# Turning the adjacency of the first three pairs on TensorE, and a new layout for the later pairs

## The chip, the cores and the metric

The kernel runs on one core of one Trainium2 chip. The metric is the device time of one execution in microseconds (us). Every kernel was checked against the reference on the chip, and all of them were correct.

## The reference, cut to what matters

```python
# x, adj: 64 graphs of 256 nodes x 256 features, float32
xc = transpose(x)
h = relu(bn(conv1d(xc, conv1_w)))
h = bn(conv1d(h, conv2_w, pad=8))              # 17 taps
x_conv = transpose(relu(h + xc))
s = x @ w_se.T + b_se                          # 3 numbers a node
dist = ...                                     # squared distances of the rows of s
A = exp(-dist) * adj                           # the mask is adj
msg = relu(x @ w_msg.T + b_msg)
x_nmp = einsum('bnm,bmd->bnd', A, msg)
gi, gh = concat(x_conv, x_nmp) @ w_ih.T + b_ih, x @ w_hh.T + b_hh
... GRU gates on gi, gh and x ...
```

The sum over m needs A with m on the partitions, that is, A turned. exp(-dist) is symmetric, so it is enough to turn adj ahead of the multiply, or the product behind it.

## The kernel before

Two graphs are a pair, four pairs are a batch, and there are eight batches. The 17-tap convolution is done by transforms: filters are made once from `taps`, stored to DRAM (`filt`) and loaded again as `wb` for the products of each batch. The program opens with a preamble (taps arrive, conv1 and the filters of the first batch), then runs the batches.

adj takes a road through DRAM. It is turned by transposing DMAs as 16-bit halves, stored (kept), loaded, and joined to float32 by two ScalarE copies:

```python
def turn_adj(i):
    HALVES[i] = (part of T, a buffer of the preamble) if i < 2 else late.tile(..., name="halves")
    for g in range(G):                                   # 2 transposing DMAs a pair
        nc.sync.dma_start_transpose(out=HALVES[i][:, g], in_=adj[G * i + g].bitcast(U16))
def keep_adj(i):                                         # 8 stores of 64 KB, rows of 512 B
    ...
def load_adj(i):                                         # 8 loads of 64 KB, issued by SP
    ...
def join_adj(i):
    for j in range(2):
        nc.scalar.copy(v[:, j], ADJH[i][:, :, :, j]...)
def affinity(i, early=False):
    ...                                                  # e = exp(-dist) on ScalarE
    nc.vector.tensor_mul(e, e, ADJ[i]...)                # times adj
def aggregate(i, join=True):                             # x_nmp; E is the moving operand
    mm(graph(p, g), MSG[i][...], E[i][:, g, c, :], ...)
    if join: join_adj(i + 1)
```

The schedule, cut to the opening and the first batch:

```python
turn_adj(0); turn_adj(1)
for j in range(PB):                          # 4 steps of the preamble
    transpose_h(j)                           # also loads x of pair j + 2: by ScalarE for j < 2, else by SP
    conv1(j); run(split_steps(j))
    for m, n in steps[j * 4:(j + 1) * 4]:
        filters(m, n, nc.sync)               # matmul, ScalarE copy to fo, store by SP
    if j < 2: keep_adj(j)
...                                          # remaining filters, stored by SP and GpSimd in turn
load_adj(0); join_adj(0)
for b in range(NB):
    message(i); products(b, 0); embed(i); products(b, 1); affinity(i)
    load_adj(i + 1); products(b, 2) ...
    aggregate(i)
    if b == 0: (load w_hh and w_ih, 2.3 MB, by GpSimd)
    message(i + 1) ... embed(i + 1); affinity(i + 1)
    if b == 0: turn_adj(2)
    products(b, 6)
    if b == 0: keep_adj(2); turn_adj(3)
    ...
    if b == 0: load_adj(2); keep_adj(3)
    aggregate(i + 1, b > 0); ... embed(i + 2)
    gates(i, 0, wait, early)                 # early: join_adj(2) if b == 0, then affinity(i + 2)
    load_adj(i + 3); turn_adj(nxt)
    if b == 0: load_y(0); load_y(1)
    ...
```

## Time and profile before

| | before |
|---|---|
| median of 4 runs | 1957.59 us (1954.89 to 1958.72) |
| span of the profiled run | 1956.3 us |
| mean granted TensorE clock | 0.977 |
| TensorE busy | 1849.5 us, 95% |
| ScalarE / GpSimd busy | 644.7 / 136.1 us |
| DMA packets | 230,650 |

The profile is of one execution. PE is TensorE, PEld its weight loads, DVE VectorE, ACT ScalarE, POOL GpSimd, SP the engine that issues most DMAs; a q behind a name (SPq) is that engine's queue of DMA issues. A line in order of time reads: start, length, engine, source line, operation, output and inputs, count, and in brackets the idle time just before and what ended it. TensorE is the bound, so what to read is its idle time: 64 of its 106.8 us lie in the first 245 us. The prediction shows those lines. In what follows h is the output of the first convolution, fo the buffer in which ScalarE puts a finished group of filters before it is stored, and y the input x as the GRU reads it again.

### The profile page before, as it was taken

How to read it: one execution, taken by the hardware profiler on the slowest of the kernel's cores; microseconds unless marked ns; L12 is line 12 of the kernel's file. 1: busy time of each engine (PE TensorE's matmuls, PEld its weight loads, DVE VectorE, ACT ScalarE, POOL GpSimd, SP SyncE). 2: the span in 40 equal slices, each digit the busy share in tenths (PEclk: the TensorE clock that was granted, in tenths of full speed). 3: DMA queues.
4: the chain of work that ended last, by engine and by line, in shares of the span. 5: the costliest groups of instructions: out<-in, count | busy, mean ns of one | idle time of the engine just before them, and what ended most of it. 6: DMA issues, size and time to landing. Idle time of an engine off the chain costs nothing.

```text
span 1956.3 us, 22266 instructions
## 1 busy us (share of the span) xinstructions
PE 1849.5 (95%) x7684; PEld 1143.7 (58%) x7684; DVE 1396.9 (71%) x2667; ACT 644.7 (33%) x1338; POOL 136.1 (7%) x204
## 2 busy tenths in 40 slices
PE   2979899999999999999999999999999999999997
PEld 1659454684448654594547744486546844477443
DVE  1758756998389865898469874898659994698522
ACT  0532343244222442224322433234422353224321
POOL 2110000000000001000000000000000000000000
PEclk8989899999999999999999999999999999998999
DMA  7777531372316514183414723165232723153020
GB/s 144 226 243 215 141 91 50 98 241 57 85 43 202 160 50 91 44 249 80 102 38 121 230 54 81 45 210 144 60 80 62 242 80 86 22 163 118 1 43 22
DMA packets 230650, 220.75 MB, mean 113 GB/s; under 512 B 90114, under 2 KB 160514, under 8 KB 230537
## 3 DMA queue, kind: packets, MB, share of 16 engines
q1 hardware_dynamic: 205516, 175.45, 31.3%
q0 software_dynamic: 20576, 40.21, 8.3%
q10 hardware_dynamic: 4445, 3.67, 0.7%
q8 instruction: 61, 1.00, 0.2%
q14 instruction: 52, 0.43, 0.1%
HBM read 156.54 MB, written 45.88 MB: 103 GB/s over the span
## 4 chain that ended last, share of the span: by engine, by line
PE 73%; DVE 11%; DMA 6%; ACT 5%; issue 4%; POOL 0%; SPq 0%; ACTq 0%; DVEq 0%; POOLq 0%
PE acc L447 63%; PE aux L447 6%; DMA wb<-filt 3%; PE aux L451 2%; DMA taps<-in_c_wT_dram 2%; PE aux L734 1%; ACT Yv L68 1%; DVE T L65 1%; DVE Yv L59 1%; DVE Yv L62 1%; ACT adj L423 1%; DVE U L65 1%; DVE PT L62 1%; DVE Sv L62 1%; DVE T L62 1%
## 5 line engine op out<-in xcount | busy, mean ns | idle before, releaser
L447 PE MATMUL acc<-hT,w_hh 128*128 128x512 f32 x768 | 365.3, 611 | 0.0
L447 PE MATMUL acc<-xnm,w_ih 128*128 128x512 f32 x768 | 354.5, 598 | 0.0
L447 PE MATMUL acc<-Yv,w_ih 128*128 128x512 f32 x768 | 340.2, 592 | 0.0
L447 PEld LDWEIGHTS acc<-xnm,w_ih 128*128 128x128 f32 x768 | 148.4, 193 | 189.2 <-issue 187.5
L447 PEld LDWEIGHTS acc<-Yv,w_ih 128*128 128x128 f32 x768 | 145.7, 190 | 184.2 <-issue 182.1
L447 PEld LDWEIGHTS acc<-hT,w_hh 128*128 128x128 f32 x768 | 145.5, 195 | 167.3 <-issue 163.0
L783 ACT ACTIVATE tr<-acc,b_rz 128x512 f32<-128x512 f32 x64 | 44.0, 687 | 552.0 <-PE acc L447 552.0
L785 DVE SCALAR_TENSOR_TENSOR gn<-tr,gn 128x512 f32<-128x512 f32 x64 | 44.2, 691 | 245.7 <-ACT tr L783 245.7
L447 PE MATMUL acc<-hT,w_c 128*128 128x512 f32 x256 | 117.8, 603 | 18.6 <-ACT hT L580 18.6
L447 PE MATMUL acc<-V,wb 128*128 128x128 f32 x1024 | 127.0, 277 | 3.5 <-DMA wb<-filt 3.3
L447 PE MATMUL aux<-w_msg,hT 128*128 128x259 f32 x512 | 121.7, 385 | 6.8 <-DVE msg L706 6.8
L447 PEld LDWEIGHTS acc<-V,wb 128*128 128x128 f32 x1024 | 121.2, 194 | 4.2 <-DMA wb<-filt 4.2
L447 PE MATMUL acc<-U,wb 128*128 128x128 f32 x1024 | 122.9, 276 | 0.0
L447 PEld LDWEIGHTS acc<-U,wb 128*128 128x128 f32 x1024 | 119.3, 192 | 3.6 <-issue 2.7
L59 DVE SCALAR_TENSOR_TENSOR V<-T,V 128x256 f32<-128x256 f32 (+2 forms) x224 | 120.4, 607 | 0.3
L447 PE MATMUL aux<-e,msg 128*128 128x256 f32 x512 | 115.8, 379 | 0.0
L447 PEld LDWEIGHTS aux<-w_msg,hT 128*128 128x128 f32 x512 | 94.5, 190 | 30.2 <-DVE msg L706 13.3
L811 POOL DMA_DIRECT2D out_dram<-y x64 | 39.4, 619 | 968.9 <-DVE y L810 939.9
L447 PEld LDWEIGHTS aux<-e,msg 128*128 128x128 f32 x512 | 95.5, 190 | 15.9 <-issue 4.3
L447 PEld LDWEIGHTS acc<-hT,w_c 128*128 128x128 f32 x256 | 48.3, 192 | 69.4 <-issue 43.2
L423 ACT COPY adj<-adjh 128x1024 uint16<-128x1024 uint16 x64 | 81.3, 1339 | 19.9 <-DMA adjh<-halves_d 14.7
L65 DVE TENSOR_TENSOR V<-h 128x512 f32<-128x512 f32 x64 | 43.8, 685 | 61.6 <-ACT h L593 61.4
(131 smaller groups left out, 2512.6 us busy)
## 6 DMA issues: line engine op xcount, KB each, us to landing
wb<-filt SPq DMA_DIRECT2D x376, 256.0 KB
adjh<-halves_d SPq DMA_DIRECT2D x256, 64.0 KB
y<-in_x_dram POOLq DMA_DIRECT2D x64, 256.0 KB, 5.8
out_dram<-y POOLq DMA_DIRECT2D x64, 256.0 KB, 5.1
x<-in_x_dram SPq DMA_DIRECT2D x60, 256.0 KB
halves_d<-halves SPq DMA_DIRECT2D x240, 64.0 KB
filt<-fo SPq DMA_DIRECT2D x26, 252.0 KB
filt<-fo POOLq DMA_DIRECT2D x10, 252.0 KB, 5.9
```

Of the source, the lines that this page charges most:

```text
L59: return self.step(out, lambda: self.v.scalar_tensor_tensor(out, x, s, y, op0=ALU.mult, op1=ALU.add))
L62: return self.step(out, lambda: self.v.tensor_add(out, x, y))
L65: return self.step(out, lambda: self.v.tensor_sub(out, x, y))
L68: return 0, lambda: self.a.mul(x, x, s)
L423: nc.scalar.copy(v[:, j], ADJH[i][:, :, :, j].rearrange("p g c n -> p (g c) n"))
L447: nc.tensor.matmul(p, w, v, **kw)
L451: nc.tensor.transpose(p, v, ident)
L734: nc.tensor.matmul(p[:, :N], ZT[rows_q, :P], ZT[rows_q, P:], start=True, stop=True)
L783: nc.scalar.activation(tr, pr, AF.Tanh, bias=b_rz[:, dc:dc + 1], scale=0.5)
L785: nc.vector.scalar_tensor_tensor(gn, tr, 1.0, gn, op0=ALU.add, op1=ALU.mult)
L811: nc.gpsimd.dma_start(out=rows(out, G * i + g), in_=row_tile(Y[i], g))
```

## The change

The intent is to take adj off the path in the opening. For the first three pairs adj is loaded as it is, and TensorE transposes the product A. From pair 3 on, one transposing DMA turns both graphs of a pair, rows are 1 KB, there are 4 stores and 4 loads a pair instead of 8 and 8, and GpSimd issues the loads. The diff, cut to its core:

```diff
+    BY_DMA = 3
     def turn_adj(i):
-        (into T if i < 2)
-        for g in range(G):
-            nc.sync.dma_start_transpose(out=HALVES[i][:, g], in_=adj[G * i + g].bitcast(U16))
+        HALVES[i] = late.tile([P, 2 * MC, W], U16, name="halves")
+        nc.sync.dma_start_transpose(out=HALVES[i], in_=adj[G * i:G * (i + 1)]...bitcast(U16))
     def keep_adj(i):
-        (8 stores, 512-byte rows)
+        for k in range(2 * MC):
+            nc.sync.dma_start(out=v[k], in_=HALVES[i][:, k])
-    def load_adj(i):
-        (8 loads by nc.sync)
+    def load_adj(i, eng=nc.gpsimd):
+        if i < BY_DMA:
+            load_rows(ADJ[i], adj, i, eng)
+            return
+        for q in range(2 * MC):
+            eng.dma_start(out=ADJH[i][:, q], in_=ADJD[i][:, q])
     def affinity(i, early=False):
...
+        AT[i] = E[i]
+        if i + 1 < BY_DMA:
+            load_adj(i + 1)
+    def transpose_a(i):
+        AT[i] = late.tile([P, 2 * MC, W], U16, name="adjh")...        # the buffer of adjh
+        for g in range(G):
+            q = aux()
+            (4 transposes of 128x128 of E[i] into q)
+            nc.scalar.copy(AT[i][:, g]..., q)
...
-    turn_adj(0)
-    turn_adj(1)
+    load_adj(0, nc.sync)
...
-        if j < 2:
-            keep_adj(j)
...
-    load_adj(0)
-    join_adj(0)
...  first batch: transpose_a(0) after products 2, transpose_a(1) after products 6,
...  transpose_a(2) after the first gates; turn_adj(3), keep_adj(3) ahead of aggregate(1)
```

More of the change, by code (lines that the diff above doesn't have):

```diff
@@ L390, in turn_adj @@
             return
-        if i < 2:
-            HALVES[i] = Tt.bitcast(U16).rearrange("p (i g k n) -> p i g k n", i=2, g=G, n=N)[:, i]
-        else:
-            HALVES[i] = late.tile([P, G, 2 * MC, N], U16, name="halves")
-        for g in range(G):
-            nc.sync.dma_start_transpose(out=HALVES[i][:, g], in_=adj[G * i + g].bitcast(U16))
+        HALVES[i] = late.tile([P, 2 * MC, W], U16, name="halves")
+        nc.sync.dma_start_transpose(out=HALVES[i],
+                                    in_=adj[G * i:G * (i + 1)].rearrange("g n m -> (g n) m").bitcast(U16))
     def keep_adj(i):
@@ L400, in keep_adj @@
             return
-        ADJD[i] = dram.tile([G, L // 2, MC, 2, NW, N], U16, name="halves_d", bufs=6)
-        v = ADJD[i].rearrange("g h c j (k a) n -> g k a (h c j) n", a=4)
-        for g in range(G):
-            for k in range(2 * MC):
-                nc.sync.dma_start(out=v[g, k], in_=HALVES[i][:, g, k])
-    def load_adj(i):
+        ADJD[i] = dram.tile([L // 2, 2 * MC, NW, W], U16, name="halves_d", bufs=6)
+        v = ADJD[i].rearrange("h q (k a) n -> k a (h q) n", a=4)
+        for k in range(2 * MC):
+            nc.sync.dma_start(out=v[k], in_=HALVES[i][:, k])
+    def load_adj(i, eng=nc.gpsimd):
         if i >= B // G:
             return
-        ADJH[i] = late.tile([P, G, MC, 2, N], U16, name="adjh")
-        v = ADJD[i].rearrange("g h c j b n -> g c j h b n")
-        for g in range(G):
-            for c in range(MC):
-                for j in range(2):
-                    nc.sync.dma_start(out=ADJH[i][:, g, c, j], in_=v[g, c, j])
+        if i < BY_DMA:
+            ADJ[i] = work.tile([P, G * MC, N], FP, name="adj")
+            load_rows(ADJ[i], adj, i, eng)
+            return
+        ADJH[i] = late.tile([P, 2 * MC, W], U16, name="adjh")
+        for q in range(2 * MC):
+            eng.dma_start(out=ADJH[i][:, q], in_=ADJD[i][:, q])
     def join_adj(i):
-        if i >= B // G:
+        if not BY_DMA <= i < B // G:
             return
         ADJ[i] = work.tile([P, G * MC, N], FP, name="adj")
-        v = ADJ[i].bitcast(U16).rearrange("p q (n j) -> p j q n", j=2)
+        v = ADJ[i].bitcast(U16).rearrange("p (g c) (n j) -> p j c g n", g=G, j=2)
+        u = ADJH[i].rearrange("p (c j) (g n) -> p j c g n", j=2, g=G)
         for j in range(2):
-            nc.scalar.copy(v[:, j], ADJH[i][:, :, :, j].rearrange("p g c n -> p (g c) n"))
+            nc.scalar.copy(v[:, j], u[:, j])
     def load_y(i):
@@ L454 @@
     PSUM, ACT = 0.2, 0.9
-    HT, MSG, E, XNM = {}, {}, {}, {}
+    HT, MSG, E, AT, XNM = {}, {}, {}, {}, {}
     def norm_steps(i):
@@ L741, in affinity, with aggregate @@
                 nc.vector.tensor_mul(e, e, ADJ[i][:, g * MC + c].rearrange("p (b h c) -> p c h b", c=MC, b=NW))
-    def aggregate(i, join=True):
+        AT[i] = E[i]
+        if i + 1 < BY_DMA:
+            load_adj(i + 1)
+    def transpose_a(i):
+        AT[i] = late.tile([P, 2 * MC, W], U16, name="adjh").bitcast(FP).rearrange("p a (b n) -> p a b n", n=N)
+        AT[i] = AT[i].rearrange("p a b n -> p (a b) n").rearrange("p (g c) n -> p g c n", g=G)
+        for g in range(G):
+            q = aux()
+            for c in range(MC):
+                for r in range(MC):
+                    transpose(q[:, c * N + r * P:c * N + (r + 1) * P], E[i][:, g, r, c * P:(c + 1) * P])
+            nc.scalar.copy(AT[i][:, g].rearrange("p c n -> p (c n)"), q)
+    def aggregate(i):
         XNM[i] = late.tile([P, DC, W], FP, name="xnm", bufs=2)
@@ L748, in aggregate @@
                 for c in range(MC):
-                    mm(graph(p, g), MSG[i][:, g, c, dc * P:(dc + 1) * P], E[i][:, g, c, :], N,
+                    mm(graph(p, g), MSG[i][:, g, c, dc * P:(dc + 1) * P], AT[i][:, g, c, :], N,
                        start=(c == 0), stop=(c == MC - 1))
             nc.scalar.activation(XNM[i][:, dc, :], p, AF.Copy)
-        if join:
-            join_adj(i + 1)
+        join_adj(i + 1)
     OT = {}
@@ L887 @@
         affinity(i)
-        load_adj(i + 1)
+        if b > 0:
+            load_adj(i + 1)
         products(b, 2)
@@ L891 @@
             finish(i - 1)
+        else:
+            transpose_a(i)
         products(b, 3)
@@ L908 @@
             load_adj(i + 2)
-        else:
-            turn_adj(2)
         products(b, 6)
         if b == 0:
-            keep_adj(2)
-            turn_adj(3)
+            transpose_a(i + 1)
         transpose_h(nxt)
@@ L930 @@
         if b == 0:
-            load_adj(2)
+            turn_adj(3)
             keep_adj(3)
-        aggregate(i + 1, b > 0)
+        aggregate(i + 1)
         message(i + 2)
@@ L939, in wait @@
             pace.flush(joined[j])
-        def early():
-            if b == 0:
-                join_adj(i + 2)
-            affinity(i + 2, True)
-        gates(i, 0, wait, early)
+        gates(i, 0, wait, lambda i=i: affinity(i + 2, True))
+        if b == 0:
+            transpose_a(i + 2)
         load_adj(i + 3)
```

## The prediction

> **What bounds the kernel now.** I read the page first, then the sums by stretch over the whole span and over the first 160 us, then the waits, then the order of time where TensorE stood still.
>
> ```profile
> span 1956.3 us, 22266 instructions
> PE 1849.5 (95%) x7684; PEld 1143.7 (58%) x7684; DVE 1396.9 (71%) x2667; ACT 644.7 (33%) x1338; POOL 136.1 (7%) x204
> ...
> DMA  7777531372316514183414723165232723153020
> ```
>
> TensorE is busy 95% of the span, which leaves 1956.3 - 1849.5 = 106.8 us for anything that only removes waits. The DMA digits (busy share of the 16 engines, slices of 48.9 us) are 7 in the first four slices, and later reach 8 only in the slice in which filters are streamed. So transfers can bound the opening; in the steady part they are mostly hidden. In windows of 49 us, TensorE is idle 38.3, 3.0, 12.5, 1.8 and 8.6 us in the first five (64 us up to 245 us), and only some 42 us in the remaining 1711. A change to the adj path must earn its money at the start.
>
> The stretches of 4 us (columns: TensorE, weight loads, VectorE, ScalarE and GpSimd busy with counts, granted TensorE clock, DMA share, GB/s):
>
> ```profile
> 32.00:36.00 4.00, 3.69 (x15) 2.44 (x13) 0.00 (x0) 0.00 (x0) 0.00 (x0) 1.00 2.16 181
> 36.00:40.00 4.00, 0.00 (x0) 0.00 (x0) 0.00 (x0) 0.00 (x0) 0.00 (x0) 0.73 0.64 112
> 40.00:44.00 4.00, 0.00 (x0) 0.00 (x0) 0.00 (x0) 0.00 (x0) 0.00 (x0) 0.50 0.80 105
> 44.00:48.00 4.00, 0.00 (x0) 0.00 (x0) 0.00 (x0) 0.35 (x1) 0.00 (x0) 0.50 1.26 115
> ...
> 132.00:136.00 4.00, 0.33 (x3) 0.14 (x2) 0.66 (x2) 0.00 (x0) 0.00 (x0) 1.00 0.78 244
> 136.00:140.00 4.00, 0.00 (x0) 0.00 (x0) 0.00 (x0) 1.37 (x2) 0.00 (x0) 0.60 0.82 242
> 140.00:144.00 4.00, 2.57 (x11) 2.21 (x12) 0.36 (x1) 3.98 (x15) 0.00 (x0) 0.50 0.44 157
> ```
>
> Two holes: 36 to 48, where every engine stands still while the DMA queues are busy but move only about 110 GB/s, and 132 to 141. The waits name a third (engine, line, what it waited for: total us, times, longest):
>
> ```profile
> ACT h L593 <- DMA taps<-in_c_wT_dram: 19.4, 1, 19.4
> ...
> ACT adj L423 <- DMA adjh<-halves_d: 14.7, 1, 14.7
> ...
> PE aux L734 <- ACT e L735: 11.1, 8, 7.9
> ...
> ACT adj L423 <- DMA halves_d<-halves: 5.2, 1, 5.2
> ```
>
> In order of time, TensorE then shows:
>
> ```profile
> 48.48 2.07 PE L447 MATMUL acc<-taps,points 119*126 119x256 f32 x4 [12.79 <-ACT h L593]
> ...
> 141.43 1.21 PE L451 MATMUL aux<-ident,z 128*128 128x128 f32 x3 [9.10 <-issue]
> ...
> 215.37 1.22 PE L734 MATMUL aux<-zT 9*128 9x256 f32 x2 [7.86 <-ACT e L735]
> ```
>
> All three belong to adj. At 36 the SP queue has just begun the four transposing DMAs of pairs 0 and 1 (issue takes 30.4 to 49.5), and ScalarE is stuck in front of its second x load, which waits for a late taps load. The 9.1 us called "issue" is really ScalarE: it sits in the join of pair 0's adj, whose load was issued only at 124 behind the filters' stores, so z, needed by that transpose, is written at 141. The 7.86 is pair 2: its adj was turned at 181, kept, loaded at 204 to 210 and joined at 212.6, in ScalarE's queue ahead of the exponential that TensorE needs.
>
> **What the Trainium skill says.** "TensorE: Matmul & The Clock Gate", Part 1, puts the array at half clock after an idle window of about 3.4 us until it has been busy again about as long. The trace agrees: the clock is 0.50 at 40 to 48 and 140 to 144, and after the third hole 512-column matmuls step 0.86 us instead of 0.43 until 222. So a hole costs more than its length. "DMA: Bandwidth & Descriptors", "Why a DMA increments its semaphore by 16 and not by 1", lets a DMA use only as many engines as divide its slowest dimension: the 119 partitions of taps give 7 of 16. The trace agrees: share 0.44 to 0.61 from 4 to 32 us, where taps are nearly all the traffic. Hence the transposes' traffic in the same rings hurts it. The same page, "Issuing engines are not separate DMA queues", says that another issuer saves only sequencer time. Moving the loads to GpSimd is then worth the SP issue (8 issues of 0.57 us, 4.6 us a pair), and SP is not what TensorE waits for: PE waits for wb 3.3 us in all.
>
> **The change, part by part.**
>
> *A, the opening.* The four transposes and 16 stores of 64 KB (SP issue 10.2 and 6.5 us) go; two plain 256 KB loads of adj come. In the built instruction lists ScalarE's second x load waited, before, for the last taps load of its own queue (landed 46.9); with fewer DMAs ahead the semaphores rotate and it now waits for SP's last taps load, whose engines landed between 35.8 and 37.8. So I expect h, written at 47.65 before, near 38. The following filter and conv steps are TensorE-bound (8.4 us per step at 52 to 72), so it carries through: about 9.5 us, less 0.5 as TensorE now meets part of the half clock while working. 9.
>
> *B, pair 0.* No join stands ahead of z. I use batch 1 as the model of an undisturbed stage: from its first product (373.24) to the aggregate of its second pair (427.71) is 54.5 us; batch 0 takes 126.81 to 193.45, 66.6, without the 0.9 us of output transposes that batch 1 holds. Gain 66.6 - 54.5 + 0.9 = 13.0, which includes the half clock.
>
> *C, pair 2.* Its adj is loaded straight, right after pair 1's multiply (189.8), by two DMAs; y loads of that size and issuer land in 5.8 us, so about 196, well before the exponential at 206. From aggregate to the first product with Yv: batch 0 193.45 to 227.99 = 34.5; batch 1 427.71 to 453.95 = 26.2. Gain 8.3.
>
> *Added.* Per pair 8 transposes of 128x128 f32: eight such (x) advance TensorE by 0.87 us (248.59 to 249.46), counted as 8 instructions; three pairs 2.6 us, on the path. The 6 copies of 128x512 out of PSUM by ScalarE, 0.59 us each (3.5), lie beside products, and 3 pairs' joins, 6 of 1.34 us (8.0), go. Pair 1's transposes come right after its products (TensorE free at 188.0), but VectorE finishes that multiply at 189.8: about 1.3 us of new wait, plus 0.5 for a PSUM buffer. The 2.3 MB of w_hh and w_ih now queue on GpSimd behind pair 1's adj load, which waits for pair 0's multiply, and so run among the wb loads instead of in the hole: 1 us. Sum 5.4.
>
> *Pair 3.* Its adjh buffer is the one in which pair 2's turned A lies, so GpSimd can load it only after pair 2's aggregate, and ScalarE's join behind that aggregate then waits about 5 to 6 us. After it (253) TensorE has matmuls until 263 before it needs a PSUM buffer that ScalarE must empty, and VectorE has 8 us of idle at 261 to 269. I count 0, with up to 3 as a risk.
>
> *Pairs 4 to 31.* The order of instructions on TensorE and VectorE is the same as before after the first batch; joins are two copies of 1,024 elements per partition as before. Halving the packets (1 KB rows) and SP's issues takes away load that is hidden anyway. 0.
>
> Net 9 + 13 + 8.3 - 5.4 = 24.9. 1958.7 - 24.9 = 1933.8.
>
> **Rivals.** (1) The holes are filled by the next limit. For it: wb loads run at 240 to 250 GB/s in the product stages, batch 0 would have to do that with 2.3 MB more on top, and from 76 to 112 the filters' stores already hold ScalarE (22.9 us of waits for filt). Against: batch 1 does the same products at full pace with only short waits. Half of B and C lost would give 1944. (2) GpSimd becomes the bound: its queue is in order, so a load of adj that waits for a buffer would hold the power for the next norm, which VectorE needs (40.4 us of waits for it already), in every batch. Against: in the lists each later load finds its buffer freed by a join an aggregate earlier. At 1 us more for each of 28 pairs: 1962. (3) The steady part gains: with adj's 512-byte packets halved and SP freed, wb comes earlier, and the dips to half clock at the middle of each batch (444, 669, 895, 1349, 1796) go. For it: 42 us of idle are there. Against: those dips follow ScalarE and VectorE around the early exponential (1.47 us waiting for zT), not a DMA. If it did happen, 15 more: 1919. (4) The taps landing stays late, since 119 partitions on 7 engines are the cause and not the transposes: A shrinks to 4, 1939.
>
> **Range and chances.** The three holes are adj's own, so a gain is nearly sure; its size depends on A (4 to 10) and on whether batch 0 reaches the pace of batch 1 (minus 8 to 0), with some 4 us either way from where the idle windows of the clock fall. I predict 1934, 8 in 10 between 1922 and 1947. The limit of 2% is 1919.5, which needs 39 us, more than the three holes hold after the additions: 0.08. Within 2%: 0.90. Slower than 1998: 0.02.
>
> **What would show it.** A: h starts near 38 and the 12.8 us wait is under 4. B: no join before the first z; TensorE has no gap over 2 us after the first products; first product to second aggregate 57 us. C: the 7.86 us wait under 1; adj of pair 2 lands before 200 less the shift of A and B. Added: 24 transposes reading e at 0.11 us each. Pair 3: a join on ScalarE waiting 5 us with no TensorE wait after it. Steady: the period of a batch stays at 225.9 us (453.95 to 679.87). I am wrong if that period changes by more than 1 us, if wb waits on TensorE exceed 5 us, or if batch 0 shows a new gap after the turned A.

## The result

| | before | changed |
|---|---|---|
| median of 4 runs | 1957.59 us | 1929.40 us (1926.87 to 1930.34) |
| span of the profiled run | 1956.3 us | 1927.1 us |
| mean granted TensorE clock | 0.977 | 0.987 |
| TensorE busy | 1849.5 us | 1845.2 us |
| ScalarE / GpSimd busy | 644.7 / 136.1 us | 640.2 / 207.9 us |
| DMA packets | 230,650 | 180,215 |

The ratio is 0.9856, with a 95% interval of 0.9839 to 0.9873. A ratio is the mean time of one kernel's runs over that of the other's in the same rounds, so it is not quite the ratio of the medians. The gain is 28 us, within 2%, and the time lies inside the predicted range, 4.6 us below the predicted value. (Some 1.1 us of that is the starting value: the prediction subtracted from the profiled run's 1958.7, and the median is 1957.59.)

The head of the page and the DMA digits of the changed kernel:

```profile
span 1927.1 us, 21948 instructions
...
PE 1845.2 (96%) x7708; PEld 1141.5 (59%) x7708; DVE 1397.0 (72%) x2667; ACT 640.2 (33%) x1338; POOL 207.9 (11%) x324
...
DMA  5777421761328331481316613174324823063010
```

There are 24 more matmuls (3 pairs of 8 transposes). The DMA digit of the first slice fell from 7 to 5.

The stretches of 4 us of the changed kernel (TensorE, weight loads, VectorE, ScalarE and GpSimd busy with counts, granted clock, DMA share, GB/s):

```profile
36.00:40.00 4.00, 0.25 (x2) 0.20 (x2) 0.00 (x0) 1.03 (x2) 0.00 (x0) 0.85 0.53 177
40.00:44.00 4.00, 4.00 (x13) 3.21 (x14) 2.50 (x4) 3.43 (x7) 0.00 (x0) 0.50 0.49 178
...
132.00:136.00 4.00, 4.00 (x38) 4.00 (x37) 3.96 (x9) 1.07 (x2) 0.25 (x1) 1.00 0.90 217
136.00:140.00 4.00, 4.00 (x29) 3.69 (x29) 3.47 (x7) 0.58 (x1) 0.00 (x0) 1.00 1.01 352
140.00:144.00 4.00, 3.62 (x25) 3.23 (x23) 3.96 (x7) 1.20 (x2) 0.00 (x0) 1.00 1.01 392
144.00:148.00 4.00, 3.03 (x25) 2.87 (x26) 3.93 (x10) 0.58 (x1) 0.00 (x0) 1.00 1.05 387
```

The first hole is now about 4 us and ends at 40 instead of 48. The second is gone: TensorE is at work through 132 to 140, at full clock. From 140 to 148 it is short of 1.3 us of work with all DMA engines busy at some 390 GB/s.

The waits of the changed kernel (who <- on whom: total us, times, longest):

```profile
POOL adjh L414 <- PE aux L447: 26.5, 1, 26.5
...
ACT h L593 <- DMA taps<-in_c_wT_dram: 10.9, 1, 10.9
ACT adj L423 <- DMA y<-in_x_dram: 10.1, 1, 10.1
...
PE aux L734 <- ACT e L735: 3.7, 8, 0.5
```

The third hole, a wait for the exponential e of 7.9 us, is down to 0.5 us at its longest. But there is a new pair of waits: GpSimd stands 26.5 us in front of the load into adjh, and ScalarE then waits 10.1 us for it (the profile names y, whose loads stand behind adj's in the same queue; the trace has adj's four landing at 230.5 to 232.4 and y's after 234, so it is adj's). In order of time:

```profile
39.80 2.07 PE L447 MATMUL acc<-taps,points 119*126 119x256 f32 x4 [3.75 <-ACT h L593]
...
186.34 0.69 PE L734 MATMUL aux<-zT 9*128 9x256 f32 x2 [0.46 <-ACT e L735]
...
222.16 2.41 POOL L414 DMA_DIRECT2D adjh<-halves_d  x4 [26.45 <-PE aux L447]
...
232.34 2.52 ACT L423 COPY adj<-adjh 128x1024 uint16<-128x1024 uint16 x2 [10.09 <-DMA y<-in_x_dram]
...
235.55 2.62 PE L447 MATMUL acc<-hT,w_hh 128*128 128x512 f32 x4 [3.63 <-ACT h L593]
```

So TensorE does stand still behind pair 3's join: 3.63 us, and the granted clock is at half from 236.8 to 240.2 afterwards.

To compare stages I took the same six points of TensorE's order of time in every kernel: the fourth group of filter matmuls (where the first hole ends), the first product (Sv with wb), the second pair's aggregate, the first product with Yv, the same product of the second batch and of the last batch. The lengths between them in us:

| stage | before | changed | gained | predicted gain |
|---|---|---|---|---|
| start to 4th filter group (part A) | 48.48 | 39.80 | 8.7 | 9 |
| to the first product ("filter stage") | 78.33 | 74.76 | 3.6 | 0 |
| to pair 1's aggregate (B, with 16 added transposes) | 66.64 | 57.78 | 8.9 | 8.5 |
| to the first Yv product (C) | 34.54 | 23.31 | 11.2 | 8.3 |
| to the next batch's (pair 2's transposes, pair 3) | 225.97 | 232.40 | -6.4 | -0.9 |
| six batches | 1361.37 | 1356.91 | 4.5 | 0 |
| the end | 140.93 | 142.17 | -1.2 | 0 |

The names A, B and C are the prediction's. The gains add up to the 29.2 us between the two spans. Each length is of one profile. In the six other kernels below that do nothing different in the filter stage (lane_one, turn_back, tensor_only, own_at, y_first, two_pairs) it is 73.2 to 76.6 us, so a difference of 2 us or less in one stage says little. The predicted 8.5 of B is 13.0 less the pair 0 and pair 1 share of the additions: 1.7 for transposes, 1.3 + 0.5 for pair 1, 1 for the weights.

### The profile page after: what moved, and what is told of

Same layout as the page of the kernel before. It is cut to its first block, busy times and chain, and to the rows that moved or that the text cites. A ratio compares the mean times of both kernels' runs of the same rounds, so it can differ in the third digit from the quotient of the medians.

```text
span 1927.1 us, 21948 instructions
## 1 busy us (share of the span) xinstructions
PE 1845.2 (96%) x7708; PEld 1141.5 (59%) x7708; DVE 1397.0 (72%) x2667; ACT 640.2 (33%) x1338; POOL 207.9 (11%) x324
## 2 busy tenths in 40 slices
DMA packets 180215, 217.63 MB, mean 113 GB/s; under 512 B 86146, under 2 KB 105858, under 8 KB 180105
## 4 chain that ended last, share of the span: by engine, by line
PE 75%; DVE 12%; ACT 5%; issue 4%; DMA 4%; POOL 1%; POOLq 0%; DVEq 0%; ACTq 0%
PE acc L447 64%; PE aux L447 7%; PE aux L451 2%; DMA taps<-in_c_wT_dram 1%; PE aux L734 1%; ACT Yv L68 1%; DVE T L65 1%; ACT adj L423 1%; DVE Yv L62 1%; DVE Yv L59 1%; DMA x<-in_x_dram 1%; DVE U L65 1%; DVE T L62 1%; DVE PT L62 1%; DVE Sv L62 1%
## 5 line engine op out<-in xcount | busy, mean ns | idle before, releaser
L447 PE MATMUL aux<-e,msg 128*128 128x256 f32 x464 | 104.9, 379 | 0.0
L447 PEld LDWEIGHTS aux<-e,msg 128*128 128x128 f32 x464 | 86.6, 190 | 14.8 <-issue 4.3
L476 POOL TENSOR_TENSOR rstd<-rstd,neg_half 128x4 f32<-128x4 f32 x32 | 36.3, 1134 | 518.8 <-DVE rstd L475 518.8
L65 DVE TENSOR_TENSOR V<-h 128x512 f32<-128x512 f32 x64 | 43.9, 685 | 63.3 <-ACT h L593 63.3
```

The costliest lines, as they stand in the source:

```text
L65: return self.step(out, lambda: self.v.tensor_sub(out, x, y))
L447: nc.tensor.matmul(p, w, v, **kw)
L476: nc.gpsimd.tensor_tensor(t["rstd"], t["rstd"], neg_half, ALU.pow)
```

## The experiments

Twelve kernels ran, in three groups of four, five rounds each. Within a group all ran on the same chip as the kernel before (medians there 1955.91, 1956.59 and 1956.08 us). Across groups I compare by ratio to that kernel; 0.001 is about 2 us. The changed kernel was not run again beside them; its row is the result above.

| kernel | median us | ratio to before, 95% | A | filter stage | B | C | next batch |
|---|---|---|---|---|---|---|---|
| changed | 1929.40 | 0.9856 (0.9839 to 0.9873) | 39.8 | 74.8 | 57.8 | 23.3 | 232.4 |
| lane_one | 1935.22 | 0.9888 (0.9874 to 0.9903) | 45.5 | 73.2 | 57.8 | 25.0 | 229.4 |
| turn_back | 1938.27 | 0.9904 (0.9888 to 0.9919) | 49.1 | 74.7 | 57.4 | 23.3 | 233.5 |
| keep_sp | 1937.52 | 0.9901 (0.9887 to 0.9915) | 39.0 | 82.8 | 57.8 | 23.3 | 229.8 |
| keep_pool | 1931.54 | 0.9871 (0.9857 to 0.9886) | 42.1 | 76.8 | 56.7 | 25.0 | 232.0 |
| layout_only | 1940.08 | 0.9915 (0.9901 to 0.9929) | 39.3 | 87.1 | 59.1 | 29.0 | 226.0 |
| layout_sp | 1956.32 | 0.9998 (0.9984 to 1.0012) | 39.7 | 87.4 | 64.0 | 34.0 | 226.2 |
| tensor_only | 1926.27 | 0.9841 (0.9828 to 0.9855) | 39.6 | 75.6 | 56.7 | 25.0 | 225.8 |
| own_at | 1924.19 | 0.9838 (0.9825 to 0.9852) | 39.9 | 76.6 | 57.1 | 23.3 | 226.8 |
| y_first | 1927.76 | 0.9851 (0.9837 to 0.9864) | 39.4 | 76.1 | 57.4 | 23.3 | 232.2 |
| two_pairs | 1928.32 | 0.9852 (0.9838 to 0.9865) | 39.3 | 75.0 | 56.9 | 27.6 | 226.0 |
| x_pool | 1928.37 | 0.9854 (0.9834 to 0.9873) | 38.5 | 79.8 | 57.0 | 23.3 | 232.2 |
| joint | 1926.64 | 0.9847 (0.9833 to 0.9861) | 38.8 | 80.9 | 58.0 | 23.3 | 228.4 |

### Which half of the change earns it: layout_only, layout_sp, tensor_only

*layout_only* is the kernel before with the new layout alone: all pairs go through DRAM, pairs 0 and 1 still turned in the preamble, loads by GpSimd.

```diff
 (the kernel before, with the changed kernel's turn, keep, load and join; no BY_DMA, no transpose_a)
+        HALVES[i] = (part of T) if i < 2 else late.tile([P, 2 * MC, W], U16, name="halves")
+        nc.sync.dma_start_transpose(out=HALVES[i], in_=adj[G * i:G * (i + 1)]...bitcast(U16))
```

> The kernel before with only the second half of the change: one transposing DMA per pair, 1 KB rows, loads by GpSimd; no pair on TensorE. If the gain is all in the first three pairs (prediction): within 4 us of the kernel before, and the period of a batch 225 to 228 us as in both. If the layout gives the steady part its 4.5 us (from the first batch's Yv products to the last's: 1361.4 before, 1356.9 after): 4 to 5 us faster than the kernel before, the same 1357 in this stretch.

It gained 16 us of the 28, which neither theory had (within 4 us, or 4 to 5 faster). None of it lies in the opening: part A is as short as in the changed kernel (39.3), but the filter stage is longer, and the first product comes at 126.4 us, against 126.8 before and 114.6 in the changed kernel. Its two transposing DMAs hold SP until 52.07, and the first store of filters goes out at 52.19. The gain is in the stages of pairs 0 and 2 (7.6 and 5.5 us) and later.

*layout_sp* has the same layout, with SP as the issuer.

```diff
-    def load_adj(i, eng=nc.gpsimd):
+    def load_adj(i, eng=nc.sync):
```

> layout_only with the adj loads issued by SP instead of GpSimd. In layout_only pair 0's stage took 59.1 us (66.6 in the kernel before), the four loads having landed 5.5 us after their issue. If 1 KB rows and half the number of DMAs did that, the stage stays within 2 us of 59; if it was the issuer, as SP is behind the filters' stores, it returns to 64 to 67 and the time grows by 5 to 7 us over layout_only.

It gained nothing: 0.9998. The time is 16 us over layout_only's (by the ratios, as the two ran in different groups), more than the 5 to 7 I had written. Pair 0's stage came back to 64.0 as that theory had it, but the stage of pair 2 lost 5.0 us as well. The stages of the two profiles hold 11.9 us; layout_sp's profiled run was the fastest of its five (1951.69), so some 4 us of the difference of the medians is in neither profile. First the loads and the join of pair 0 in layout_only (GpSimd), in order of time:

```profile
124.64 2.41 POOL L411 DMA_DIRECT2D adjh<-halves_d  x4 [0.28 <-issue]
...
129.47 2.56 ACT L420 COPY adj<-adjh 128x1024 uint16<-128x1024 uint16 x2 [5.46 <-DMA adjh<-halves_d]
```

Then the same in layout_sp:

```profile
124.59 3.03 SPq L411 DMA_DIRECT2D adjh<-halves_d  x4
...
138.22 2.52 ACT L420 COPY adj<-adjh 128x1024 uint16<-128x1024 uint16 x2 [14.03 <-DMA adjh<-halves_d]
```

The four loads, the bytes and the time of issue are the same, yet the join waits 14.0 us instead of 5.5. So fewer and longer rows alone are not what helps; the change of issuer is. (Whether GpSimd would help the old 512-byte rows as much was not run.) What this pair of runs does not separate is the issuer itself from the order that comes with it. With GpSimd as the issuer, the 2.3 MB of w_hh and w_ih stood in its queue behind the adj loads of pairs 0 and 1 and were issued at 134.6. With SP, GpSimd issued them at 124.0, in the same microsecond as adj, and the DMA engines were full from 128 to 136 (share 1.03). In the stage of pair 2 the place in the queue differs again: SP issued the loads at 201.3, behind six wb loads, and GpSimd at 189.9.

*tensor_only* takes the other half: three pairs on TensorE, but the old layout for the rest (two transposing DMAs, 512-byte rows, 8 stores and 8 loads by SP). The turned A lies in a buffer of y, as in own_at below.

> TensorE transposes A of pairs 0 to 2 (their turned A kept in a buffer of the y rotation, as in own_at), but the later pairs keep the old layout: two transposing DMAs a pair, 512-byte rows, 8 stores and 8 loads by SP. The layout alone (layout_only) was worth 16 of the change's 28 us. If the two halves of the change are independent, the TensorE half gives the other 12: about 1945. If they overlap, because either one empties the opening and the join of pair 0, this kernel should come near own_at, within 4 us of it, at 1922 to 1932; h again near 38 to 39 and pair 0's stage near 58.

```diff
 (own_at, with the kernel before's turn, keep, load and join for pairs >= 3)
+        for g in range(G):
+            for c in range(MC):
+                for j in range(2):
+                    nc.sync.dma_start(out=ADJH[i][:, g, c, j], in_=v[g, c, j])
```

It reached 0.9841, 2 us from own_at (0.9838), which has the new layout, and well inside its interval. So the TensorE half alone, with that buffer, is worth all of it; the new layout adds nothing that can be measured on top, for all its 38,500 fewer packets (218,729 against 180,216). The two halves overlap in the stages of pairs 0 and 2, where either takes the wait for a join out of the way; the 12 us of the opening come with the TensorE half alone.

### What shortened the opening: lane_one, turn_back, keep_sp, keep_pool

In the built instruction lists the DMAs that SP and ScalarE issue share eight completion semaphores, taken in turn, and an issue first waits for the DMA that used its semaphore before. *lane_one* adds a store of 8 KB on SP, right behind the new load of adj, which shifts the turn by one:

```diff
     load_adj(0, nc.sync)
+    lane_d = dram.tile([4, 16, P], FP, name="lane_d")
+    nc.sync.dma_start(out=lane_d[0], in_=ident[:16, :])
```

> The changed kernel plus one 8 KB store from SP behind the adj loads of pair 0, which does nothing but turn the rotation of DMA semaphores by one, so that ScalarE's second x load waits again for the last taps load of ScalarE's own queue (landed at 46.9 before the change, 45.1 after it). If stage A was won by the rotation of the semaphores: h moves from 39.0 back to about 45.5, and the time rises by 5 to 7 us, to about 1935. If it was won because the transposes no longer crowd the taps: h stays at 39 to 40 and the time within 1 us of the changed kernel.

ScalarE's loads of x, and h behind them, in lane_one:

```profile
37.47 7.12 ACTq L377 DMA_DIRECT2D x<-in_x_dram  x2
44.71 1.45 ACT L593 ACTIVATE h<-acc,bn_shift,bn_scale 128x512 f32<-128x512 f32 x2 [17.21 <-DMA x<-in_x_dram]
```

In the changed kernel the two issues took 2.98 us (35.87 to 38.85) and h came at 38.97. One store of 8 KB moves h by 5.7 us and the time by 6 us (0.9888 against 0.9856). Traffic of 8 KB is no likely cause, and the lists name the other: ScalarE's second load waits for ScalarE's own last taps load, as it did before, and in the changed kernel for a taps load of SP's (landed at 38.2, when ScalarE's landed at 45.1).

*turn_back* puts the four transposing DMAs of pairs 0 and 1 back, into a buffer that nobody reads:

```diff
     load_adj(0, nc.sync)
+    junk = Tt.bitcast(U16).rearrange("p (i k n) -> p i k n", i=4, n=N)
+    for k in range(4):
+        nc.sync.dma_start_transpose(out=junk[:, k], in_=adj[k].bitcast(U16))
```

> The changed kernel with the four transposing DMAs of pairs 0 and 1 put back at their old place, their result unused; the second x load waits for the last taps load of ScalarE's queue, as before the change. If the rotation made stage A: the same as the run with one store, within 2 us, h at 46 to 47. If the traffic of the transposes made it: 7 us or more over the changed kernel while the run with one store shows nothing.

h came at 48.28 and the ratio is 0.9904: part A is undone altogether, and the time is 3 us over lane_one's, where I had written 2 at most. It moves the turn of the semaphores too, so it measures both. Layout_only still has two transposing DMAs of the same bytes in the opening, but with fewer issues its h came at 38.5. The landings on that semaphore tell the two apart: ScalarE's last taps load landed at 46.9 before, 47.5 in turn_back and 47.3 in layout_only, all with the transposes, and at 43.9 in lane_one and 45.1 in the changed kernel, without them. So the transposes delay that load by some 2 to 4 us, and they delay h only where h waits for that load.

*keep_sp* puts the 16 stores of the preamble back (64 KB each, 512-byte rows):

```diff
+    junk_d = dram.tile([2, 8, 32, 4, 2 * P], U16, name="junk_d")
...
             filters(m, n, nc.sync)
+        if j < 2:
+            for k in range(8):
+                nc.sync.dma_start(out=junk_d[j, k].rearrange("c a n -> a c n"), in_=ident.bitcast(U16))
```

> The changed kernel with 16 stores of 64 KB in 512-byte rows from SP, after the filters of the first two steps, as the kernel before had them (source: the identity, result unused). The filter stage from the fourth group of filters to the first product took 78.3 us before and 74.8 after, which the prediction had as equal. If SP's issue and these stores cost the 3.6 us: 78 us in this stage, time about 1933. If the filter stage was shorter for another reason (where the stores of filters fall against the reads of filters): 75 us, time within 1.5 us of the changed kernel.

*keep_pool* is the same with nc.gpsimd.

> Like keep_sp (16 stores of 64 KB put back into the opening, 512-byte rows), but issued by GpSimd. keep_sp lengthened the filter stage from 74.8 to 82.8 us. If the traffic did that, it is 82 to 84 here too; if it was SP's 16 issues ahead of the filters' stores, it is 74 to 77.

With SP the filter stage took 82.8 us (78 was expected, had the stores cost just the 3.6), with GpSimd 76.8. SP's queue in keep_sp shows why (start, length of the issuing):

```profile
43.55 1.80 SPq L624 DMA_DIRECT2D filt<-fo  x4
45.45 9.62 SPq L871 DMA_DIRECT2D junk_d<-ident  x8
55.17 2.04 SPq L624 DMA_DIRECT2D filt<-fo  x4
57.26 6.79 SPq L871 DMA_DIRECT2D junk_d<-ident  x8
64.16 1.33 SPq L377 DMA_DIRECT2D x<-in_x_dram  x2
```

Eight stores hold SP for 9.6 and 6.8 us, and the filters' stores and x come behind them; ScalarE waits 21.9 us for free fo buffers from 30 to 125, and 14.1 in keep_pool. So most of the 8 us is SP's queue. The test is not clean: GpSimd issued its first eight stores at 23 to 29, before h, so they lie elsewhere in time, and part A grew by 2.3 us there.

### Pair 3 and the buffer: own_at, y_first, two_pairs

*own_at* puts the turned A into a free buffer of y, so that adjh is free for pair 3:

```diff
-        AT[i] = late.tile([P, 2 * MC, W], U16, name="adjh").bitcast(FP)...
+        AT[i] = late.tile([P, G * MC, N], FP, name="y", bufs=2).rearrange("p (g c) n -> p g c n", g=G)
```

> The turned A of pairs 0 to 2 lies in a buffer of the y rotation, no longer in the one pair 3's adj is loaded into. Theory: pair 3's load then starts before pair 2's aggregate, its join waits for nothing, and the TensorE wait of 3.63 us with the half clock after it (5.5 us in all) goes: 1923 to 1925, with the first batch period back at 226 to 227 instead of 232.4. Rival: y, whose buffer is now taken, comes late instead and ScalarE or VectorE wait there: no gain, 1929.

In order of time in own_at, the load and the join of pair 3:

```profile
196.97 2.43 POOL L414 DMA_DIRECT2D adjh<-halves_d  x4
...
223.43 2.52 ACT L423 COPY adj<-adjh 128x1024 uint16<-128x1024 uint16 x2
```

The load goes out 25 us earlier, the join waits for nothing, TensorE has no wait over 0.5 us from 180 to 260, and the stage is 226.8 instead of 232.4. The 5.6 us are gained back in that stage. In time the ratio is 0.9838 against 0.9856, some 3.5 us, and the intervals overlap: the stage shows the effect, the totals do not settle its size. Nor does the stage of one profile: in the other kernels with the old buffer it is 229.4 to 233.5 us, with the free buffer 225.8 in tensor_only and 228.4 in joint.

*y_first* issues GpSimd's loads of y ahead of pair 3's adj:

```diff
         if b == 0:
             transpose_a(i + 2)
+            load_y(0)
+            load_y(1)
         load_adj(i + 3)
         turn_adj(nxt)
-        if b == 0:
-            load_y(0)
-            load_y(1)
```

> GpSimd issues the two y loads before pair 3's adj load. Theory that y's 1 MB beside it stretched that load from 5 to 6 us to 10.25 us: the adj now lands about 6 us after its issue, the join comes some 4 us earlier and TensorE's 3.63 us wait goes: 5 us faster, 1924. Rival, that the load of adj is slow of itself or waits only for its buffer: the landing stays near 10 us after the issue, and the time within 2 us of the changed kernel.

In y_first, pair 3's load and join:

```profile
222.68 2.36 POOL L414 DMA_DIRECT2D adjh<-halves_d  x4 [24.05 <-issue]
...
231.28 2.52 ACT L423 COPY adj<-adjh 128x1024 uint16<-128x1024 uint16 x2 [8.51 <-DMA adjh<-halves_d]
```

Without y behind it the load still took 8.6 us from first issue to join, against 10.2 in the changed kernel and some 5 in own_at at 197. The stage stayed at 232.2. So y behind it is at most a small part; what the start at 197 instead of 222 changes is shown by own_at. What else stretches the load at 222 was not tested.

*two_pairs* gives pair 2 back to the DMA road (new layout, GpSimd's loads, the old schedule):

```diff
-    BY_DMA = 3
+    BY_DMA = 2
...  turn_adj(2) after affinity(1), keep_adj(2) and turn_adj(3) after products 6,
...  load_adj(2) ahead of aggregate(1), join_adj(2) ahead of affinity(2); no transpose_a(2)
```

> Only pairs 0 and 1 go through TensorE; pair 2 is turned, kept, loaded and joined on the schedule of the kernel before, but as one transposing DMA with 1 KB rows loaded by GpSimd. It gives up the shorter stage from the aggregate of pair 1 to the first Yv product (23.3 becomes 29, as in layout_only) and pair 2's transposes (0.9), and should get back pair 3's TensorE wait of 3.63 us and the half clock after it (5.5 together), as no turned A holds that buffer. Theory that pair 2 on TensorE is about even: within 3 us of the changed kernel. Theory that pair 2 on TensorE pays: 5 us slower or more.

C became 27.6 (4.3 lost), the next batch 226.0 (6.4 won), and the time 0.9852: no difference. With pair 3 waiting for its buffer, the third pair on TensorE is worth nothing. With own_at's buffer it would, by these stages, be worth the 4.3; own_at, run beside it in the same group, is 4.1 us faster by the medians (1924.19 against 1928.32), but the intervals overlap.

### Attempts at a faster opening: x_pool, joint

In *x_pool* GpSimd loads x of pairs 2 and 3, so nothing in ScalarE's queue waits for a DMA ahead of h:

```diff
-            load_x(i + 2, nc.scalar if i < 2 else nc.sync)
+            load_x(i + 2, nc.gpsimd if i < 2 else nc.sync)
```

> The changed kernel with x of pairs 2 and 3 loaded by GpSimd, so that ScalarE's queue has no x load that waits for a taps load ahead of h. Theory that this wait is what holds h at 39.0: h at 32 to 34 and up to 6 us gained, 1923. Rival, that the taps landings (the last at 43 to 45) or the x arrival bound the opening next: h earlier but the later taps groups wait, gain 2 us or less.

h came at 33.8, but the filter stage grew from 74.8 to 79.8 and the time did not move. SP's queue and its waits in x_pool show where it went:

```profile
37.61 16.50 SPq L624 DMA_DIRECT2D filt<-fo  x8
```

```profile
SPq L624 <- DMA taps<-in_c_wT_dram: 13.3, 3, 9.8
```

The filters' stores, which SP issues, stand 9.8 us behind a taps load whose semaphore they reuse: ScalarE's last one, which lands at 50.4, and the third store goes out at 50.43. ScalarE runs out of fo buffers at 47 and waits 4.1 us. SP waited for the same load in the changed kernel, too (it landed at 45.1, the first store went out at 45.21), but there ScalarE waited for no fo buffer in front of its next copy at 49.47. So with h earlier the late taps hold the next step.

*joint* is own_at and x_pool together, with w_hh and w_ih issued before the first batch:

```diff
+    nc.gpsimd.dma_start(out=w_hh, ...)
+    nc.gpsimd.dma_start(out=w_ih, ...)
     for b in range(NB):
...
-        if b == 0:
-            nc.gpsimd.dma_start(out=w_hh, ...)
-            nc.gpsimd.dma_start(out=w_ih, ...)
```

> The candidate that should beat both: own_at, x_pool and the loads of w_hh and w_ih issued before the first batch. If the three add up (5.5, up to 6 and 1.3 us): 1916 to 1920. If one of them only moves a wait, 1922 to 1926.

It missed: 1926.64, with a filter stage of 80.9. It is no better than own_at, and no run beats the changed kernel by more than the intervals allow; own_at has the lowest ratio.

## Why the prediction was right, and where its steps failed

**A** held in size, 8.7 us for 9, and in its main cause: the turn of the semaphores, as stated. lane_one undoes 5.7 us of it with 8 KB. The rest goes with the earlier landing of the taps without the transposes, as the prediction had also said; but the load that they delayed is ScalarE's, and that the two meet in the same rings is not shown. Rival 4 fell, though its premise held: ScalarE's last taps load still landed late, at 45.1 for 46.9, and h no longer waited for it.

That the step "carries through" because TensorE bounds what follows was not reason enough. In layout_only the same 39.3 us of part A gained nothing by the first product (126.4 for 126.8), and with keep_sp's 16 stores the first product comes at 121.8. It carries through in the changed kernel because the transposes and the 16 stores of adj, which had stood in SP's queue ahead of the filters' stores, are gone as well; there the filter stage even gained 3.6 us. The stores cost the more the earlier h comes: without them and with h late, turn_back takes 74.7 us for the 78.3 before, and with h early keep_sp takes 82.8 for 74.8.

**B** held: the stage came to 57.8 where I had said 57, and no join stands ahead of the first z. The 1.3 us of new wait expected at pair 1's transposes did not come: TensorE's transposes waited for e twice, 0.4 us in all. The 1 us for the weights among the wb loads came as 0.52 + 0.82 us of waits for wb, between 141 and 147. Of rival 1 only that came.

**C** was undersized: 11.2 for 8.3. The model for it, batch 1 of the kernel before, holds a wait of 1.47 us for zT and a stretch at half clock. In the changed kernel the longest wait of that stage is the 0.46 us for e shown above, and the clock stayed at full.

**Pair 3** is the step that failed most plainly. "I count 0, with up to 3 as a risk" became a TensorE wait of 3.63 us and, with the half clock, 5.6 us of stage by own_at. The buffer was foreseen, and the wait of the load for it (26.5 us) is as stated. The load then took 10.2 us, so ScalarE waited 10.1 us at the join and not 5 to 6; the join ended at 234.9, and the matmuls that I had counted on ran out before ScalarE emptied the PSUM buffer, where their results go. So one of my own signs of being wrong appeared, a new gap of TensorE after the turned A of batch 0. What the Trainium skill says in "TensorE: Matmul & The Clock Gate", Part 1 (half clock after an idle window of about 3.4 us), on which the prediction drew, held here too: an idle stretch of 3.63 us was followed by half clock for 3.4 us (236.8 to 240.2).

**The steady part** showed 4.5 us less over six batches, 0 predicted. The half clock in that stretch went from 30.7 to 23.9 us, which I estimate at (30.7 - 23.9) / 2 = 3.4 us. But lane_one, keep_sp and own_at, all with the new layout, have the 1361 us of before there (with 37.5 us of half clock), and layout_sp, which gains nothing overall, has 1357. So it is no gain of the change, and rival 3's dips moved and did not go; what sets them is open. By the letter my sign for this part failed, too: the period that I named is 227.57 us for 225.92, over the 1 us that I allowed. It says little, as the periods of the kernel before alone run from 225.83 to 228.16. Together C, the filter stage and the steady part made up for pair 3, and the sum came within 4.6 us: partly by luck.

**The issuer.** I had said that moving the loads to GpSimd is worth only SP's issue time, which nobody waits for. In the changed kernel that is right (tensor_only against own_at: 2 us, inside the intervals). As a statement on the layout in general it is wrong: with pairs 0 to 2 on the DMA road the issuer, with the order that comes with it, was worth 16 us (layout_only against layout_sp). I had read which engine waits for SP, and not what stands in SP's queue ahead of the loads or beside them in the DMA engines. Rival 2 fell: GpSimd's busy time rose by 72 us, and the batches did not lengthen.

## What to carry to other kernels

Before giving a gain to a transfer's bytes, look at which earlier DMA its issue waits for: adding or removing an unrelated DMA can move that wait (here by 5.7 us, with a store of 8 KB). When a turned or temporary tile borrows another tile's buffer, follow that buffer to its next user; here it cost 5.6 us in the stage. Follow a shortened wait to the next step, too: in layout_only 9 us won at h were worth nothing by the first product, with SP held by its transposes. And run each half of a two-part change alone: here one half had all of the gain, the other 16 of the same 28 us, and of those nothing with another issuer.

## What the Trainium skill lacked or had wrong

- No page has it that completion semaphores taken in turn couple DMAs that have nothing to do with each other. An extra store of 8 KB moved h from 38.97 to 44.71 us and cost 6 us; in x_pool SP stood 9.8 us behind a taps load that ScalarE had issued.
- "DMA: Bandwidth & Descriptors", "Issuing engines are not separate DMA queues", says that issuing from several engines only saves sequencer time. Here the same four loads, issued at the same time, were waited for 5.5 us from GpSimd and 14.0 us from SP, and the kernels differ by 16 us. What a place in an issuer's queue, and what is issued beside it, can cost is not in that section; the runs do not separate it from an effect of the issuer itself.
- "DMA: Bandwidth & Descriptors", "Anatomy of one DMA — SWDGE (gpsimd) path", fits a DMA from GpSimd as 2.0 us plus its bytes over 436 GB/s; an estimate from that is 2.3 us for the 128 KB of one adjh load. The profile has a median of 5.6 us from issue to landing for these, among other traffic, and 8.6 to 10.2 us for the four loads of pair 3 at 222.
